# Turning gathered rows and weighed values by transposing transfers of 16-bit halves, in an attention and mixture-of-experts block

## The chip, the cores and the metric

The kernel runs on one core of one Trainium2 chip. A core has a matrix engine (TensorE, PE in the profile, with weight loads shown as PEld), a vector engine (DVE), a scalar engine (ACT), GpSimd (POOL) and a queue engine (SP) that here only issues DMAs. Each engine takes its own instructions in order and waits on semaphores for the others. The metric is the device time of one execution in microseconds, as a median over several runs.

## The reference

The block normalizes x (16 sequences of 256 tokens, 256 features, float32), and adds causal attention and a mixture of experts, both computed on the same normalized rows, to x.

```python
x = L0_attn_hidden_states                                  # (16, 256, 256)
xn = _layernorm(x, axis=-1)
# attention: 16 heads of 16, rotary positions
qkv = jnp.einsum('bsd,ed->bse', xn, w_qkv) + b_qkv
q = q * cos + _rotate_half(q) * sin                        # k likewise
scores = jnp.einsum('bhqd,bhkd->bhqk', q, k) / norm        # masked to j <= i
out = jnp.einsum('bhqk,bhkd->bhqd', softmax(scores), v)
# experts: 8 of them, inner width 512, weights from a router
probs = jax.nn.softmax(xn @ router_w.T, axis=-1)
w = _top_p_weights(probs, 0.9)                             # 0 for experts not kept
for e in range(8):
    y = (silu(xn @ gate_w[e].T) * (xn @ up_w[e].T)) @ down_w[e].T
    moe = moe + y * w[:, e:e + 1]
x = x + out + moe
```

## The kernel before

It has two stages.

**Attention.** Tokens lie in 32 tiles of 128; a sequence b has two of them (NQ = 2). A sequence takes 8 steps (PPS = 8): step i works on one pair of heads p of one chunk c of four heads, so there are 128 steps. A step multiplies queries with keys (products, tile s), takes the maxima of its rows on DVE (maxima, L593, which writes top), and, LAG = 11 steps later, does the same products the other way round (tile st) with the maximum folded in, and exponentiates them on ACT (probabilities, pr). Every second step four heads are weighed: weigh (L625) multiplies pr by the values into a PSUM tile o, whose row 16 of each head's 32 is the sum of the weights, and copies it to oT on ACT. One step later finish (L641) turns oT by two TensorE transposes into the PSUM tile ot, takes the reciprocal rs of the sums and the product at on DVE, and POOL adds at to xs. Between these, prep_jobs prepares the next sequence: prep_norm (L422 on) normalizes a tile into xn on ACT and stores it to the DRAM tensor rows; prep_xnT turns it; prep_qk, prep_v, rotation and prep_turn make queries, keys and values. The router's parts (router, L509) are taken one a step from an iterator, todo; the last of them go on to dispatch, which finds the slots of the first experts' tokens and gathers their rows.

The tensor rows holds, for each token, 256 normalized features and 8 expert weights, 1,056 bytes.

**Experts.** Each expert has room for 1,472 tokens (CAP), in 12 blocks of 128 (the last one of 64), worked off in four groups of up to three blocks. For a group, fetch gathers the rows of its blocks by an indirect DMA of POOL into xg, two groups ahead (AHEAD = 2). turn_in (L801) turns a block by two TensorE transposes into the PSUM tile xt and copies it to xT, on DVE or ACT by turns. expand (L813) multiplies xT by gate and up weights into gu, and makes hT. contract multiplies by the down weights into py, scales by the token's weight into ys, and scatters ys into out by an indirect DMA that adds. In one pass of the loop, for q = 0 to 3, come expand of group i, contract of block q of group i - 1, and turn_in of block q of group i + 1. load_expert(e + 1) puts three loads of 512 KB on SP at the first group of expert e; wd of an expert lies in one of two buffers. The search for slots (find, L309) multiplies selected rows into a tile seen and counts on DVE; eight waves of it (find_wave) run in the experts' stage. A last work item, the 33rd, takes an overfull expert's remaining tokens.

**PSUM.** Two pools: ps_m with two buffers (pq, pv, o, ot, xnt, top, upc, seen, xt, py) and ps_sc with three (s, st, gu).

**Order.** The program text gives priorities; the framework's scheduler writes the order of each engine's queue, and adds the semaphores. tc.issue_after and tc.high_priority bend that order in places.

Of the kernel before, what the change touches and what calls it, by code (L numbers as in the profile page):

```python
# [10 lines left out]
F32 = mybir.dt.float32  # L11
BF16 = mybir.dt.bfloat16
I32 = mybir.dt.int32
AF = mybir.ActivationFunctionType
# [9 lines left out]
MASKED = -3.0e38  # L24
CAP = 1472
# [6 lines left out]
def kernel(  # L32
# [27 lines left out]
    rt = rows[: NT * P, :].rearrange("(t p) c -> p t c", p=P)  # L60

# [247 lines left out]
    def find(h, js, to, numbers, token, name):  # L309
# [4 lines left out]
        for r in range(4):  # L314
            rows_r = slice(32 * r, 32 * r + 32)
            seen = ps_m.tile([P, 3, P + 2], F32, tag="m", name=f"seen_{name}_{r}")
# [6 lines left out]
            for i, j in enumerate(js):  # L323
                less = gat.tile([P, P], F32, tag="less", name=f"less_{name}", bufs=2)
# [22 lines left out]
    def find_wave(h, w):  # L347
# [9 lines left out]
        yield from find(h, js, holds, mine, to, f"{h}_{w}")  # L357
# [5 lines left out]
    def fetch_block(token, name, n=P):  # L363

        xg = gat.tile([P, D + E], F32, tag="xg", name=f"xg_{name}")
        nc.gpsimd.indirect_dma_start(  # L366
            out=xg[:n, :], out_offset=None, in_=rows,
            in_offset=bass.IndirectOffsetOnAxis(ap=token, axis=0),
        )
        return xg  # L370
# [21 lines left out]
    with tc.tile_pool(name="prep", bufs=2) as prep, tc.tile_pool(  # L392
# [21 lines left out]
        seqs, stored, sums, unturned, normed = {}, {}, {}, [], {}  # L414
# [7 lines left out]
        def prep_norm(b):  # L422

            normed[b] = []
            for qi in range(NQ):
                t = b * NQ + qi
                xn = prep.tile([P, D], F32, tag="xn", name=f"xn_{t}", bufs=6)
# [4 lines left out]
                stored[b] = nc.sync.dma_start(rt[:, t, :D], xn)  # L432
                normed[b].append(xn)

# [152 lines left out]
        def maxima(b, c, p, sc):  # L587

            for j in range(2):
                for qi in range(NQ):  # L590
                    lo, hi = (0, P) if qi == 0 else (P, W)
                    junk = probs.tile([P, 2 * P], F32, tag="junk", name=f"junk_{b}", bufs=2)
# [32 lines left out]
        def weigh(b, c, prs):  # L625
# [11 lines left out]
            oT = probs.tile([P, S], F32, tag="oT", name=f"oT_{b}_{c}", bufs=2)  # L637
            nc.scalar.copy(oT, o)
            return oT

        def finish(b, c, oT):  # L641
            ot = ps_m.tile([P, NQ, P], F32, tag="m", name=f"ot_{b}_{c}")
            for qi in range(NQ):
                nc.tensor.transpose(ot[:, qi, :], oT[:, ts(qi, P)], ident)
            ot = ot.rearrange("p q (h d) -> p (q h) d", d=HP)
# [37 lines left out]

        for t0 in (0, NQ):
# [29 lines left out]
        def dispatch():  # L714
# [3 lines left out]
            for w in range(AHEAD):  # L718
                yield from find_wave(0, w)
# [6 lines left out]
        while late < len(steps) or weighed or finished:  # L726
# [21 lines left out]
            if i < len(steps):  # L748
# [9 lines left out]
                for job in todo_now:  # L758
                    job()
                if i == PPS - 1:  # L760
# [23 lines left out]
            for _ in range(1 if i < len(steps) else 2):  # L784
                next(todo, None)
# [5 lines left out]
            for k in finished.pop(i, ()):  # L791
                finish(steps[k][0], steps[k][1], held.pop(k))
        at_once(todo)
# [213 lines left out]
```

## Time and profile before

| | us |
|---|---|
| median of 9 runs | 964.18 (960.73 to 969.74) |
| the profiled execution, its own time | 962.85 |
| its span, first to last instruction | 961.1 |
| granted TensorE clock, mean | 0.992 |

The page cuts the span into 40 slices of 24 us; each digit is a busy share in tenths:

```profile
PE   6988999999999999999999999999999999999996
...
DVE  3968788878787878551111433322111111212110
ACT  3254744565444444422222212112222222222221
POOL 5424233333433332434545344434544545446523
PEclk9979999999999999999999999999999999999999
DMA  7024100010200000112343322333432423424313
```

Attention ends near slice 17, at about 415 us, where DVE's digits fall from 8 to 1. The costliest groups that the change touches, by line, with busy time in all:

| line | what | count | mean ns | busy us |
|---|---|---|---|---|
| L644 | PE transposes ot of oT, 128x128 | 128 | 277 | 25.0 |
| L805 | PE transposes xt of xg, 128x128 | 176 | 276 | 34.1 |
| L805 | the same, 64 rows | 16 | 248 | 2.7 |
| L638 | ACT copy oT, 128x256 | 64 | 372 | 23.8 |
| L647 | DVE reciprocal rs, 128x8 | 64 | 200 | 12.8 |
| L649 | DVE product at, 128x128 | 64 | 291 | 18.6 |
| L806 | DVE copy xT, 128x256 | 57 | 424 | 24.2 |
| L806 | ACT copy xT, 128x256 | 32 | 364 | 11.6 |
| L318 | PE products seen, 128x130 | 208 | 290 | 27.2 |

Busy time counts overlapping instructions of one engine once, so it is below count times mean.

### The profile page before, as it was taken

The numbers are of one execution on the slowest core, as the hardware profiler recorded it, in microseconds if no ns is written. First come the engines' busy times: TensorE is split into PE (matmuls) and PEld (weight loads), VectorE is DVE, ScalarE is ACT, GpSimd is POOL, SyncE is SP. The second block draws the span as 40 slices with busy tenths as digits, with TensorE's granted clock in tenths as the row PEclk, the third lists the DMA queues.
The fourth block names the chain that finished last, engine by engine and source line by source line (L and its number), as shares of the span: only waits on it lengthen the run. The fifth ranks groups of instructions, "written<-read, shape, count | busy, mean of one in ns | idle before, by whom it ended". The sixth has DMA issues, their size and how long they took to land. (4 is left out here: it accounts for less than half of the span.)

```text
span 961.1 us, 17451 instructions
## 1 busy us (share of the span) xinstructions
PE 921.0 (96%) x6564; PEld 613.0 (64%) x6564; DVE 446.6 (46%) x2059; ACT 317.9 (33%) x606; POOL 400.5 (42%) x473
## 2 busy tenths in 40 slices
PE   6988999999999999999999999999999999999996
PEld 3555556566656666556766766666766667667675
DVE  3968788878787878551111433322111111212110
ACT  3254744565444444422222212112222222222221
POOL 5424233333433332434545344434544545446523
PEclk9979999999999999999999999999999999999999
DMA  7024100010200000112343322333432423424313
GB/s 248 13 89 155 59 13 13 14 57 25 89 24 14 13 13 14 42 56 48 56 105 55 89 58 43 66 79 55 90 72 45 108 53 60 106 51 91 56 20 39
DMA packets 46366, 57.53 MB, mean 60 GB/s; under 512 B 9313, under 2 KB 37601, under 8 KB 46273
## 3 DMA queue, kind: packets, MB, share of 16 engines
q0 software_dynamic: 19360, 29.81, 17.0%
q1 hardware_dynamic: 26912, 26.52, 8.6%
q8 instruction: 54, 0.88, 0.4%
q14 instruction: 40, 0.32, 0.1%
HBM read 32.14 MB, written 24.17 MB: 59 GB/s over the span
## 5 line engine op out<-in xcount | busy, mean ns | idle before, releaser
L871 POOL DMA_INDIRECT out<-ys,tokens x96 | 151.6, 1579 | 248.6 <-ACT ys L865 188.0
L825 DVE TENSOR_TENSOR hT<-act,gu 128x384 f32<-128x384 f32 (+2 forms) x132 | 69.9, 530 | 328.4 <-ACT act L824 328.3
L819 PE MATMUL gu<-xT,wg 128*128 128x384 f32 (+1 forms) x512 | 182.4, 477 | 0.0
L860 PE MATMUL py<-wd,hT 128*128 128x256 f32 (+1 forms) x768 | 181.8, 380 | 0.0
L819 PE MATMUL gu<-xT,wu 128*128 128x384 f32 (+1 forms) x512 | 181.0, 475 | 0.0
L593 DVE CUSTOM_DVE_ANT_0 junk<-s,mask 128x128 f32<-128x128 f32 (+1 forms) x512 | 152.5, 352 | 35.7 <-PE s L580 34.9
L860 PEld LDWEIGHTS py<-wd,hT 128*128 128x128 f32 (+1 forms) x768 | 141.7, 186 | 41.6 <-issue 3.8
L824 ACT ACTIVATE act<-gu 128x384 f32<-128x384 f32 (+2 forms) x132 | 62.2, 471 | 297.1 <-PE gu L819 292.0
L622 ACT ACTIVATE pr<-st 128x768 f32<-128x768 f32 x128 | 103.7, 812 | 115.7 <-PE st L617 114.7
L819 PEld LDWEIGHTS gu<-xT,wu 128*128 128x128 f32 x512 | 96.3, 190 | 59.4
L580 PE MATMUL s<-kT,qT 32*128 32x128 f32 (+1 forms) x1024 | 120.1, 353 | 3.8 <-ACT pr L622 2.7
L580 PE MATMUL st<-qT,kT 32*128 32x128 f32 (+1 forms) x1024 | 121.7, 361 | 2.0 <-DVE top L593 1.6
L366 POOL DMA_INDIRECT xg<-rows,tokens x96 | 94.2, 981 | 46.5 <-issue 21.0
L819 PEld LDWEIGHTS gu<-xT,wg 128*128 128x128 f32 x512 | 88.9, 190 | 37.1
L653 POOL TENSOR_TENSOR xs<-xs,at 128x128 f32<-128x128 f32 x64 | 29.8, 466 | 141.3 <-DVE at L649 141.3
L865 ACT ACTIVATE ys<-py,xg 128x256 f32<-128x256 f32 x96 | 45.4, 473 | 121.8 <-PE py L860 120.6
L580 PEld LDWEIGHTS st<-qT,kT 32*128 32x128 f32 x1024 | 68.9, 188 | 25.0 <-issue 18.4
L580 PEld LDWEIGHTS s<-kT,qT 32*128 32x128 f32 x1024 | 68.2, 188 | 9.1 <-ACT pr L622 3.8
L632 PE MATMUL o<-pr,va 128*32 128x256 f32 (+1 forms) x1024 | 57.0, 337 | 11.2 <-DVE at L649 10.0
L450 PE MATMUL pq<-wqkv_sb,xnT 128*128 128x512 f32 x128 | 63.9, 623 | 1.5 <-DVE logits L476 0.8
L489 POOL TENSOR_TENSOR kp<-qk,rot 128x256 f32<-128x256 f32 x32 | 24.2, 757 | 90.3 <-DVE rs L647 51.2
L611 POOL TENSOR_TENSOR qT<-qT,topT 128x256 f32<-128x256 f32 x64 | 50.8, 826 | 22.5 <-ACT topT L609 22.5
(156 smaller groups left out, 952.1 us busy)
## 6 DMA issues: line engine op xcount, KB each, us to landing
rows<-xn SPq DMA_DIRECT2D x32, 128.0 KB, 1.8
wg<-in_wg SPq DMA_DIRECT2D x8, 512.0 KB, 4.0
wu<-in_wu SPq DMA_DIRECT2D x8, 512.0 KB, 5.0
wd<-in_wd SPq DMA_DIRECT2D x8, 512.0 KB, 3.9
out<-xs SPq DMA_DIRECT2D x16, 256.0 KB, 2.2
xs<-in_x SPq DMA_DIRECT2D x3, 1024.0 KB, 11.3
rows<-zeros POOLq DMA_DIRECT2D x1, 1716.0 KB, 8.4
out<-zeros POOLq DMA_DIRECT2D x1, 1664.0 KB, 12.7
```

The lines of the kernel that those rows point to most:

```text
L366: nc.gpsimd.indirect_dma_start(out=xg[:n, :], out_offset=None, in_=rows, in_offset=bass.IndirectOffsetOnAxis(ap=token, axis=0),)
L450: nc.tensor.matmul(pq, xnT[:, c, ts(qi, P)], wqkv_sb[:, c, : 2 * D], start=(c == 0), stop=(c == DC - 1),)
L580: opened = nc.tensor.matmul(sc[:, j, to], left[rows, c, lhs], right[rows, c, lhs if first else slice(0, S)], start=first, stop=False, skip ...
L593: ins = nc.vector.tensor_tensor_reduce(junk[:, : hi - lo], sc[:, j, lo:hi], mask[:, 2 * P - (hi - lo) :], -1.0, -MASKED, ALU.add, ALU.min, ...
L611: nc.gpsimd.tensor_tensor(qT[:, c, :], qT[:, c, :], topT, ALU.add)
L622: nc.scalar.activation(pr, sc[:, :, :W], AF.Exp)
L632: nc.tensor.matmul(o[32 * hh : 32 * hh + 32, kc * P :], v[:, kc, 4 * c + hh, :], pr[:, j, : 2 * P] if kc == 0 else pr[:, j, 2 * P :], star ...
L819: nc.tensor.matmul(gu[:, j, :w], w_sb[:, c, ts(i, P)], xT[:, c, :w], start=(c == 0), stop=(c == DC - 1),)
L824: nc.scalar.activation(act[:, :w], gu[:, 0, :w], AF.Silu)
L825: nc.vector.tensor_tensor(hT[:, i, :w], act[:, :w], gu[:, 1, :w], ALU.mult)
L860: nc.tensor.matmul(py[:n, :], hT[:, i, k * P : k * P + n], d_sb[:, i, :], start=(i == 0), stop=(i == IC - 1),)
L871: ins = nc.gpsimd.indirect_dma_start(out=out, out_offset=bass.IndirectOffsetOnAxis(ap=token, axis=0), in_=ys[:n, :], in_offset=None, compu ...
```

## The change

Transposes on TensorE at two places give way to DMA transposes issued on SP. Such a transfer moves elements of 16 bits, so a float32 row is handled as its low and its high halves, side by side, and the halves are put together again by a copy behind the transfer.

- finish: oT is written by ACT as two planes of halves, [128, 2, 256]; a transfer turns it into half; POOL copies 17 of each head's 32 columns, halves interleaved, into the SBUF tile ot; rs and at read that.
- turn_in: rows keeps the 256 features as 256 low and then 256 high halves; a gather brings them into xg (16-bit type, same bytes); a transfer turns xg into half, six buffers; the DVE or ACT copy to xT interleaves the halves.
- store: the store to rows leaves prep_norm; a new function makes the planes of halves by an ACT copy and issues the store, for one waiting tile a step, in six of eight steps.
- find takes its pool as an argument; the eight waves in the experts' stage use ps_sc instead of ps_m.
- The router's next part is taken at the end of a step, behind weigh and finish, instead of ahead of them.
- 32 transposes of the identity (warm) stand at the start of TensorE's work.
- Fewer buffers: xn 6 to 5, less 2 to 1, junk 2 to 1.

```diff
+WARM = 32
...
+    halves = rows.bitcast(U16)
+    ht = halves[: NT * P, :].rearrange("(t p) c -> p t c", p=P)
...
-    def find(h, js, to, numbers, token, name):
+    def find(h, js, to, numbers, token, name, pool, tag):
...
-            seen = ps_m.tile([P, 3, P + 2], F32, tag="m", name=f"seen_{name}_{r}")
+            shape = [P, 4 * P] if pool is ps_m else [P, 2, 4 * P]
+            seen = pool.tile(shape, F32, tag=tag, name=f"seen_{name}_{r}")
+            seen = (seen if pool is ps_m else seen[:, 0, :])[:, : 3 * (P + 2)]
+            seen = seen.rearrange("p (i s) -> p i s", i=3)
...
-        xg = gat.tile([P, D + E], F32, tag="xg", name=f"xg_{name}")
+        xg = gat.tile([P, 2 * (D + E)], U16, tag="xg", name=f"xg_{name}")
         nc.gpsimd.indirect_dma_start(
-            out=xg[:n, :], out_offset=None, in_=rows,
+            out=xg[:n, :], out_offset=None, in_=halves,
...
-                stored[b] = nc.sync.dma_start(rt[:, t, :D], xn)
                 normed[b].append(xn)
+                unstored[t] = xn
+
+        def store(t):
+
+            half = prep.tile([P, 2, D], U16, tag="half", name=f"half_{t}")
+            nc.scalar.copy(
+                half, unstored.pop(t).bitcast(U16).rearrange("p (d h) -> p h d", h=2)
+            )
+            stored[t // NQ] = nc.sync.dma_start(
+                ht[:, t, : 2 * D], half.rearrange("p h d -> p (h d)")
+            )
...
-            oT = probs.tile([P, S], F32, tag="oT", name=f"oT_{b}_{c}", bufs=2)
-            nc.scalar.copy(oT, o)
+            oT = probs.tile([P, 2, S], U16, tag="oT", name=f"oT_{b}_{c}", bufs=2)
+            nc.scalar.copy(oT, o.bitcast(U16).rearrange("p (s h) -> p h s", h=2))
             return oT
 
         def finish(b, c, oT):
-            ot = ps_m.tile([P, NQ, P], F32, tag="m", name=f"ot_{b}_{c}")
-            for qi in range(NQ):
-                nc.tensor.transpose(ot[:, qi, :], oT[:, ts(qi, P)], ident)
-            ot = ot.rearrange("p q (h d) -> p (q h) d", d=HP)
+            half = probs.tile([P, 2, NQ * 4, HP], U16, tag="oh", name=f"oh_{b}_{c}", bufs=2)
+            nc.sync.dma_start_transpose(
+                half.rearrange("p h (q g) d -> p (h q) (g d)", q=NQ),
+                oT.rearrange("p h s -> p (h s)"),
+            )
+            ot = probs.tile([P, NQ * 4, HD + 2], F32, tag="ot", name=f"ot_{b}_{c}", bufs=2)
+            both = ot.rearrange("p g d -> p (g d)").bitcast(U16)
+            both = both.rearrange("p (g d h) -> p h g d", g=NQ * 4, h=2)
+            nc.gpsimd.tensor_copy(both[:, :, :, : HD + 1], half[:, :, :, : HD + 1])
...
+        warm = ps_sc.tile([P, 2, 4 * P], F32, tag="sc", name="warm")
+        for _ in range(WARM):
+            nc.tensor.transpose(warm[:, 0, :P], ident, ident)
...
+                if i % PPS not in (4, 5):
+                    for t in list(unstored)[:1]:
+                        store(t)
...
-            for _ in range(1 if i < len(steps) else 2):
-                next(todo, None)
             k = i - 1
...
                 finish(steps[k][0], steps[k][1], held.pop(k))
+            for _ in range(1 if i < len(steps) else 2):
+                next(todo, None)
...
-            tp = ps_m.tile([P, DC, P], F32, tag="m", name=f"xt_{name}_{i}")
-            for c in range(DC):
-                nc.tensor.transpose(tp[:, c, :n], xg[:n, ts(c, P)], ident[:n, :n])
+
+            half = hid.tile([P, 2 * DC, P], U16, tag="half", name=f"xt_{name}_{i}", bufs=6)
+            nc.sync.dma_start_transpose(half[:, :, :n], xg[:n, : 2 * D])
+            both = xT.rearrange("p c t -> p (c t)").bitcast(U16)
+            both = both.rearrange("p (c t h) -> p h c t", c=DC, h=2)
             (nc.scalar.copy if i % 2 else nc.vector.tensor_copy)(
-                xT[:, :, i * P : i * P + n], tp[:, :, :n]
+                both[:, :, :, i * P : i * P + n],
+                half.rearrange("p (h c) t -> p h c t", h=2)[:, :, :, :n],
             )
...
-                at_once(find_wave(*wave))
+                at_once(find_wave(*wave, ps_sc, "sc"))
```

More of the change, by code (lines that the diff above doesn't have):

```diff
@@ L13 @@
 I32 = mybir.dt.int32
+U16 = mybir.dt.uint16
 AF = mybir.ActivationFunctionType
@@ L323, in find @@
             for i, j in enumerate(js):
-                less = gat.tile([P, P], F32, tag="less", name=f"less_{name}", bufs=2)
+                less = gat.tile([P, P], F32, tag="less", name=f"less_{name}", bufs=1)
                 nc.vector.tensor_scalar(
@@ L345, with find_wave @@
     assert WAVES[-1] == (NB - 1,)
-    def find_wave(h, w):
+    def find_wave(h, w, pool, tag):
         js = WAVES[w]
@@ L356, in find_wave @@
         yield
-        yield from find(h, js, holds, mine, to, f"{h}_{w}")
+        yield from find(h, js, holds, mine, to, f"{h}_{w}", pool, tag)
     def at_once(parts):
@@ L412, in statistics @@
             )
-        seqs, stored, sums, unturned, normed = {}, {}, {}, [], {}
+        seqs, stored, sums, unturned, normed, unstored = {}, {}, {}, [], {}, {}
         def open_seq(b):
@@ L426, in prep_norm @@
                 t = b * NQ + qi
-                xn = prep.tile([P, D], F32, tag="xn", name=f"xn_{t}", bufs=6)
+                xn = prep.tile([P, D], F32, tag="xn", name=f"xn_{t}", bufs=5)
                 nc.scalar.activation(
@@ L591, in maxima @@
                     lo, hi = (0, P) if qi == 0 else (P, W)
-                    junk = probs.tile([P, 2 * P], F32, tag="junk", name=f"junk_{b}", bufs=2)
+                    junk = probs.tile([P, 2 * P], F32, tag="junk", name=f"junk_{b}", bufs=1)
                     ins = nc.vector.tensor_tensor_reduce(
@@ L718, in dispatch @@
             for w in range(AHEAD):
-                yield from find_wave(0, w)
+                yield from find_wave(0, w, ps_m, "m")
                 fetched[w] = fetch(*work[w])
@@ L792 @@
                 finish(steps[k][0], steps[k][1], held.pop(k))
+            for _ in range(1 if i < len(steps) else 2):
+                next(todo, None)
+        for t in list(unstored):
+            store(t)
         at_once(todo)
@@ L829, in weights_of @@
             if e < E:
-                return xg[:n, D + e : D + e + 1]
+                return xg.bitcast(F32)[:n, D + e : D + e + 1]
             picked = gat.tile([P, E], F32, tag="picked", name="picked", bufs=1)
             weight = gat.tile([P, 1], F32, tag="weight", name="weight", bufs=1)
-            nc.vector.tensor_tensor(picked, xg[:, D:], pick, ALU.mult)
+            nc.vector.tensor_tensor(picked, xg.bitcast(F32)[:, D:], pick, ALU.mult)
             nc.vector.tensor_reduce(weight, picked, AX.X, ALU.add)
@@ L941 @@
                     tile_rows = bass.ts(t, P)
-                    xg = gat.tile([P, D + E], F32, tag="xg", name=f"xg_o{e}")
-                    nc.sync.dma_start(xg, rows[tile_rows, :])
+                    xg = gat.tile([P, 2 * (D + E)], U16, tag="xg", name=f"xg_o{e}")
+                    nc.sync.dma_start(xg, halves[tile_rows, :])
                     xo = open_in(f"o{e}")
```

## The prediction

> **What bounds the kernel now.** I read first the busy times of the page, then busy times by stage, then the timeline of one stretch of each stage, then what the DMA queue waits for, last the durations of the nearest operations.
>
> ```profile
> PE 921.0 (96%) x6564; PEld 613.0 (64%) x6564; DVE 446.6 (46%) x2059; ACT 317.9 (33%) x606; POOL 400.5 (42%) x473
> ```
> ```profile
> 200.00:250.00 50.00, 47.61 (x592) 30.58 (x592) 37.38 (x192) 27.07 (x49) 17.72 (x27) 1.00 0.12 37
> ...
> 700.00:800.00 100.00, 100.00 (x388) 68.30 (x388) 18.84 (x38) 22.60 (x50) 48.12 (x39) 1.00 0.35 70
> ```
> The columns are PE, weight load, DVE, ACT, POOL, granted clock, DMA share, GB/s. TensorE is the bound in both stages: 95% busy in attention (about 25 to 415 us), 100% in the experts (about 415 to 955 us). But DVE is at 75% in attention and under 20% in the experts, so only attention has a second engine close behind.
>
> **What is removed.** Transposes on TensorE, in two places.
>
> ```profile
> 204.89 0.38 PE L644 MATMUL ot<-ident,oT 128*128 128x128 f32 x2
> ...
> 205.20 0.49 PE L580 MATMUL st<-qT,kT 32*128 32x128 f32 x4
> ...
> 205.47 0.20 DVE L647 RECIPROCAL rs<-ot 128x8 f32<-128x8 f32 x1
> ...
> 205.77 0.29 DVE L649 TENSOR_TENSOR at<-ot,rs 128x128 f32<-128x128 f32 x1
> ...
> 206.15 0.45 POOL L653 TENSOR_TENSOR xs<-xs,at 128x128 f32<-128x128 f32 x1 [4.00 <-DVE at L649]
> ```
> ```profile
> 759.73 1.89 PE L860 MATMUL py<-wd,hT 128*128 128x256 f32 x8
> 761.46 0.38 PE L805 MATMUL xt<-ident,xg 128*128 128x128 f32 x2
> 761.68 1.46 PE L819 MATMUL gu<-xT,wg 128*128 128x384 f32 x4
> 762.97 1.45 PE L819 MATMUL gu<-xT,wu 128*128 128x384 f32 x4
> ```
> Matmuls overlap, so the price of a pair is how far it pushes the next one: 205.20 - 204.89 = 0.31 us in attention (this holds for nearly all 64 pairs), 761.68 - 761.46 = 0.22 in the experts. That is 64 x 0.31 = 19.8 us, and 97 x 0.22 = 21.3, with 0.5 more for the eight pairs of 64 rows, which push 0.28: 41.6 us in all. Against the profiled execution (962.85 us, span 961.1 and 1.75 around it; the median of the runs is 1.3 above it) that alone would give 921.
>
> **What is added, and what hides it.**
>
> ```profile
> rows<-xn SPq DMA_DIRECT2D x32, 128.0 KB, 1.8
> ...
> xg<-rows,tokens POOLq DMA_INDIRECT x96, 2.8
> out<-ys,tokens POOLq DMA_INDIRECT x96, 3.8
> ```
> *Transfers.* 160 and one transposing transfers of 128 KB on SP. The trace has none. Bounds: the plain 128 KB store lands in 1.8 us, the scatter with addition in 3.8; I take 2.8, the gather, also 128 pieces of 1 KB spread over partitions. The Trainium skill (VectorE: DVE Perf Modes, "The three transpose paths") gives 1309 ns for one 128x128 16-bit square by DMA and prefers TensorE where PSUM will do; four such squares would be an estimate of 5.2 us, three blocks 15.7 us of a group of about 16, and the experts would gain next to nothing. The same skill (Advanced Engine Details and Errata, "X-Bar Transpose (TRN2)") calls such transfers as fast as ordinary ones, which would put them at the store's row; no row here decides between the two.
>
> *Finishing in attention.* The copy oT grows from 256 to 512 elements per partition.
> ```profile
> L611 POOL TENSOR_TENSOR qT<-qT,topT 128x256 f32<-128x256 f32 x64 | 50.8, 826 | 22.5 <-ACT topT L609 22.5
> ...
> L638 ACT COPY oT<-o 128x256 f32<-128x256 f32 x64 | 23.8, 372 | 57.3 <-PE o L632 57.0
> ...
> L505 ACT COPY qT<-qt 128x512 f32<-128x512 f32 x32 | 18.6, 580 | 0.8 <-PE qt L503 0.8
> ```
> So 372 becomes 580 ns, 64 x 0.21 = 13 us of ACT. POOL gets 64 copies of 272 halves: no less than its memset of 256 (0.31 us), no more than L611's 0.83; I take 0.55, 35 us. The stores' halving is 32 ACT copies of 512 elements, 0.58 each, 19 us. Over 390 us ACT goes from 27 to 31 of 50 and POOL from 18 to 22: covered. A late ACT copy can hold a pr, which TensorE's o needs: 0 to 32 x 0.58 = 19 us, I take 2, as ACT idles 23 of 50.
>
> The reciprocal now starts about 0.58 + 2.8 + 0.55 = 3.9 us after o, where it was some 2. The wait stands in DVE's queue: behind rs lie the next maxima (L593), and TensorE's products wait for these through three score banks. It costs nothing if the reciprocal is placed late enough. The scheduler does place by readiness: load_expert(0) stands at step 20 of the program, about 81 us by the first finishes (66.9 us at step 15, 84.0 at step 21), and the DMA queue issued it at 58.1. If its idea of a transfer is short, DVE stands. Bounds per finish: 0, and all the extra 1.9 us (122 us in all). DVE idles 12.6 of 50, 1.5 us per finish, which takes most of a small miss; I take 0.12, 8 us. One wait goes: ot held one of two PSUM buffers until at was done, and TensorE waited for that 12 us in attention (o 10.0 in 7 waits, xnt 2.1 in 3, by the table of waits). DVE's lateness stands behind these too and may come back elsewhere: gain 0 to 12, I take 6.
>
> *Turning in the experts.* Copies of 512 halves, 0.58 (ACT) to 0.69 us (DVE's 512-wide add), instead of 0.36 and 0.42: under 30 us on engines at 19 and 23 of 100. The transfers go on SP, where weights wait:
> ```profile
> SPq L658 <- POOL xs L653: 141.5, 16, 21.6
> ...
> SPq L87 <- PE xt L805: 85.2, 6, 16.2
> ```
> The wd load waits up to 16.2 us for the last contraction of the expert before. At 766.32 it goes out and TensorE reaches the next group at 769.08, 2.8 us later; three transfers behind it (4 issues of 0.37, 2.8, a copy 0.6: 4.9) would cost 2.1 at each of 6 changes, 13 us, up to 24 if they land in 3.8 and DVE has a backlog. I take 0: gathers run two groups ahead, six buffers hold two groups, so the transfers are ready long before wd is, and readiness orders the queue.
>
> *Slot search and the change of stages.* The search takes gu's three banks. Each tile holds one for a copy of 0.16 and three comparisons of 0.43, 1.45 us; later waves have py (5.2 us a group) to fill in, the first two have not: 8 x 1.45 less 8 x 6 x 0.12 of their own matmuls, 5.8 us at most. At 415 us the first xT copy waited for POOL's last xs (1.7 us): that chain grows by 2 and a transfer of 2.8 follows before the first gu. Bounds 0 to 11; I take 6.
>
> *Start.* 32 transposes of ident at some 0.25 us (the first four, at 6.18, took 1.09) run from 1.7 to about 9.7 us, 3.5 past the first real one; the first xnt, pq and pv took 0.45 + 1.88 + 0.89 = 3.2 longer than their next ones, at a granted clock of 1.00, so that much may come back. I take 0, bounds -3.2 to +3.5. One junk and one less buffer (same engine, in order), five xn of which a sequence uses two, gathers of the same 1,056 bytes a row: 0. The router's parts move behind rs and at on DVE and their store behind a transposing transfer on SP; what they make is needed only by the dispatch from step 115 on, so 0 before it, and at most one finish's 1.9 us there, which is in the 6.
>
> **Sum:** 962.85 - 41.6 - 6 + 8 + 2 + 6 = 931.3, say 931; its own range 916 to 955.
>
> **Rivals.**
> 1. *Nothing lost.* All 12 us of the bank's waits come back and no new wait shows: 962.85 - 41.6 - 12 = 909, up to 916 with some of the 6 at the change of stages. For it: the experts' slack; against: DVE at 75%. 0.12.
> 2. *SP order.* Transfers stand behind wd: 931 + 13 to 24, 944 to 955. For it: the 16 us waits; against: the reordering shown. 0.12.
> 3. *DVE stands in attention* (slower). Place: rs at each of 64 finishes. Gain left before it, 41.6 + 6 - 8 = 39.6 us, so it decides from 0.62 us each. At 1.2 us each, two thirds of the 1.9: 962.85 - 39.6 + 77 = 1000. For it: in-order queue, two added hops (DMA, POOL); against: DVE's idle time. 0.23.
> 4. *The transfers bound the experts.* At 5.4 us each, the longest gather, and none overlapping, a group needs 16.2 against 15.9 before: 32 x 0.3 = +10, attention even: 973. For it: DMA engines a third busy already; against: other transfers overlap. 0.10.
>
> **How the numbers follow.** Forecast 0.43, rivals as above. A change under 0.5% (4.8 us) can't be told from none here. Faster takes the forecast's 0.43 and the 0.12 of each of rivals 1 and 2: 0.67; same 0.05, that part of rival 3 that stays near its point of decision; slower the rest of it, 0.18, and rival 4's 0.10: 0.28. Below 912 and above 985 lie about 2 in 10: the upper end takes in rival 4 and the lower part of rival 3.
>
> **What would show it.** Right: no transposes on TensorE for ot and xt; an expert's four groups in some 60.9 us, where 63.5 is seen now; transfers landing in 2 to 4 us; eight attention steps in 22 to 23 us, now 23.7. Wrong: a wait of rs or junk for POOL's new copy, a share of DMA wait before gu, or a TensorE idle over 6 us near 415.

## The result, and the profile after

The changed kernel takes 1043.91 us (median of 10 runs, 1040.65 to 1048.77) against 964.18 us: a ratio of 1.083, with a 95% interval of 1.080 to 1.085. It is slower by some 80 us, where 931 was forecast. The kernel before itself has some executions of 975 to 979 us at a mean granted clock of 0.975 to 0.979, 4 of 13 beside e1 to e4 and 8 of 13 beside e13 and e14 (median there 975.19), so the ratios of those last two are not used.

The page of the kernel after, busy times and slices (its span is 1043.8 us, so a slice is 26 us):

```profile
PE 933.1 (89%) x6274; PEld 608.4 (58%) x6274; DVE 476.0 (46%) x2059; ACT 360.8 (35%) x638; POOL 436.4 (42%) x537
...
PE   6987696978788988888599999999999999999997
...
DVE  3866657876767777864331114343311111111111
...
PEclk8989879999899999976689999999999999999999
```

Most of TensorE's nines in attention (slices 2 to 16) have become sixes to eights, and the clock now shows sixes to eights in nine slices, where before only the third slice was below 9. TensorE has 290 fewer instructions and yet is busy 12 us longer.

Four marks cut each span into five stages that are nearly the same work in every kernel (a few products move across a mark with the order of the queues): the first and the last maxima on DVE, and the first and the last of the six loads of gate weights for experts 2 to 7, each of which waits for TensorE's last gate product two experts earlier. The spans by stage, in us, with the difference from before (from marks rounded to 0.1 us):

| kernel | start | attention | last maxima to end of expert 0 | five experts | rest | span | clock in the third stage |
|---|---|---|---|---|---|---|---|
| before | 24.1 | 367.2 | 88.7 | 335.2 | 145.9 | 961.1 | 0.98 |
| after | 29.7 (+5.6) | 448.2 (+81.0) | 104.9 (+16.1) | 320.2 (-15.0) | 140.8 (-5.0) | 1043.8 (+82.7) | 0.82 |
| e1_finish_only | -0.7 | +87.2 | +19.2 | 0.0 | +0.4 | +106.1 | 0.81 |
| e2_turn_only | +1.1 | +25.8 | +15.5 | -14.6 | -4.1 | +23.7 | 0.87 |
| e3_late_1 | +4.7 | +21.8 | +16.7 | -15.0 | -4.8 | +23.3 | 0.82 |
| e4_idle_transfer | +0.4 | +0.2 | +15.6 | 0.0 | +0.5 | +16.7 | 0.84 |
| e5_one_buffer | -1.0 | +28.6 | +3.1 | +0.7 | +0.5 | +31.9 | 0.98 |
| e6_two_buffers | +4.7 | +61.6 | +10.8 | -15.0 | -4.0 | +58.0 | 0.87 |
| e7_late_two | +4.9 | +18.6 | +12.3 | -15.0 | -4.4 | +16.4 | 0.83 |
| e8_best | +0.9 | +18.1 | +14.3 | -14.9 | -4.2 | +14.1 | 0.80 |
| e9_experts_part | +3.1 | +3.9 | +10.0 | -14.9 | -4.9 | -2.8 | 0.86 |
| e10_fill_later | +0.4 | +18.9 | +12.5 | -14.9 | -4.7 | +12.3 | 0.83 |
| e11_filled_14 | +1.2 | +7.4 | +7.5 | -14.9 | -4.5 | -3.3 | 0.91 |
| e12_filled_28 | +0.7 | +7.5 | +8.1 | -14.9 | -4.5 | -3.1 | 0.91 |
| e13_filled_68 | +0.8 | +7.1 | +10.7 | -14.9 | -4.9 | -1.3 | 0.95 |
| e14_fill_at_64 | +9.6 | +9.0 | +12.6 | -14.9 | -5.0 | +11.3 | 0.83 |

These are single profiled executions; a kernel's median can lie some us from its profiled one (e5's by 9, e4's by 4). The experts gain nearly what was forecast, 20 us. Attention loses four times that.

**What attention waits for.** Of the table of waits of the kernel after (waiting instruction, what ended the wait, us in all, times, longest):

```profile
POOL ot L667 <- DMA oh<-oT: 203.7, 51, 13.0
...
DVE rs L669 <- POOL ot L667: 97.4, 53, 8.0
...
PEld st L597 <- DVE top L610: 49.3, 48, 6.9
...
PE st L597 <- DVE top L610: 34.5, 34, 6.0
```

POOL's wait costs nothing by itself. The next line does: the reciprocal rs stands 97.4 us in DVE's queue, 71.5 of them ahead of the last maxima (57 finishes, 1.25 us each) and 26.0 behind them (7 finishes). The last two lines are TensorE's side: its products wait for maxima that stand behind rs. In the kernel before rs waited for TensorE, and all of it behind the last maxima, and the products waited 4.8 and 1.6 us:

```profile
DVE rs L647 <- PE ot L644: 7.2, 5, 2.0
...
PEld st L580 <- DVE top L593: 4.8, 17, 1.0
```

One finish in the timeline of the kernel after, one of the slow ones (start, us, engine, line, in brackets the idle time before it and what ended it):

```profile
216.96 0.58 ACT L655 COPY oT<-o 128x512 uint16<-128x512 uint16 x1
...
220.28 0.38 SPq L566 DMA_DIRECT2D rows<-wts  x1
...
220.77 1.19 SPq L660 DMA_TRANSPOSE oh<-oT  x1
...
224.55 0.50 POOL L667 COPY ot<-oh 128x272 uint16<-128x272 uint16 x1 [5.04 <-DMA oh<-oT]
225.09 0.20 DVE L669 RECIPROCAL rs<-ot 128x8 f32<-128x8 f32 x1 [3.28 <-POOL ot L667]
225.21 0.24 DVE L610 CUSTOM_DVE_ANT_0 junk<-s,mask 128x128 f32<-128x128 f32 x1
...
226.06 0.38 PE L597 MATMUL st<-qT,kT 32*128 32x128 f32 x2 [3.26 <-DVE top L610]
```

oT is ready at 217.54, but the transfer goes out at 220.77: in SP's queue it stands behind the router's store of weights, which waits for DVE. From oT to the reciprocal it is 7.5 us here. By the median of the 64 finishes the transfer goes out 0.06 us behind oT, and from oT to the reciprocal it is 4.30 us, where before it was 2.25; 7 transfers go out more than 2 us late. Here rs comes between maxima of one step, so TensorE waits 3.26 us for the maxima behind it.

### The profile page after: what moved, and what is told of

Same layout as the page of the kernel before. It is cut to its first block, busy times and chain, and to the rows that moved or that the text cites. A ratio compares the mean times of both kernels' runs of the same rounds, so it can differ in the third digit from the quotient of the medians.

```text
span 1043.8 us, 17154 instructions
## 1 busy us (share of the span) xinstructions
PE 933.1 (89%) x6274; PEld 608.4 (58%) x6274; DVE 476.0 (46%) x2059; ACT 360.8 (35%) x638; POOL 436.4 (42%) x537
## 2 busy tenths in 40 slices
DMA packets 131902, 78.12 MB, mean 75 GB/s; under 512 B 94848, under 2 KB 123136, under 8 KB 131808
## 5 line engine op out<-in xcount | busy, mean ns | idle before, releaser
L610 DVE CUSTOM_DVE_ANT_0 junk<-s,mask 128x128 f32<-128x128 f32 (+1 forms) x512 | 180.0, 351 | 32.4 <-PE s L597 20.0
L597 PE MATMUL st<-qT,kT 32*128 32x128 f32 (+1 forms) x1024 | 134.8, 382 | 36.6 <-DVE top L610 34.5
L597 PE MATMUL s<-kT,qT 32*128 32x128 f32 (+1 forms) x1024 | 129.7, 373 | 20.0 <-ACT pr L639 14.0
L853 PEld LDWEIGHTS gu<-xT,wg 128*128 128x128 f32 x512 | 97.0, 191 | 45.6 <-issue 4.2
L597 PEld LDWEIGHTS st<-qT,kT 32*128 32x128 f32 x1024 | 74.2, 199 | 78.7 <-DVE top L610 49.3
L667 POOL COPY ot<-oh 128x272 uint16<-128x272 uint16 x64 | 32.5, 508 | 203.7 <-DMA oh<-oT 203.7
L373 POOL DMA_INDIRECT xg<-rows,tokens x96 | 99.2, 1034 | 41.5 <-issue 27.7
L467 PE MATMUL pq<-wqkv_sb,xnT 128*128 128x512 f32 x128 | 67.9, 656 | 21.3 <-DVE logits L493 14.8
L839 DVE COPY xT<-xt 128x512 uint16<-128x512 uint16 x65 | 25.6, 437 | 96.5 <-PE gu L853 95.8
L649 PE MATMUL o<-pr,va 128*32 128x256 f32 (+1 forms) x1024 | 66.4, 376 | 0.1
L669 DVE RECIPROCAL rs<-ot 128x8 f32<-128x8 f32 x64 | 13.0, 203 | 97.7 <-POOL ot L667 97.4
```

Source lines behind the costliest of these rows:

```text
L373: nc.gpsimd.indirect_dma_start(out=xg[:n, :], out_offset=None, in_=halves, in_offset=bass.IndirectOffsetOnAxis(ap=token, axis=0),)
L467: nc.tensor.matmul(pq, xnT[:, c, ts(qi, P)], wqkv_sb[:, c, : 2 * D], start=(c == 0), stop=(c == DC - 1),)
L597: opened = nc.tensor.matmul(sc[:, j, to], left[rows, c, lhs], right[rows, c, lhs if first else slice(0, S)], start=first, stop=False, skip ...
L610: ins = nc.vector.tensor_tensor_reduce(junk[:, : hi - lo], sc[:, j, lo:hi], mask[:, 2 * P - (hi - lo) :], -1.0, -MASKED, ALU.add, ALU.min, ...
L649: nc.tensor.matmul(o[32 * hh : 32 * hh + 32, kc * P :], v[:, kc, 4 * c + hh, :], pr[:, j, : 2 * P] if kc == 0 else pr[:, j, 2 * P :], star ...
L853: nc.tensor.matmul(gu[:, j, :w], w_sb[:, c, ts(i, P)], xT[:, c, :w], start=(c == 0), stop=(c == DC - 1),)
```

## The experiments

**First four: which part loses.** Two theories stood against each other: W, that the reciprocal's wait in DVE's queue makes the loss, and T, that the transfers themselves disturb the other work.

e1_finish_only: the kernel before with the new weigh and finish, and one junk buffer; rows, turn_in, search, router and start as before.

```diff
-            nc.scalar.copy(oT, o)
+            nc.scalar.copy(oT, o.bitcast(U16).rearrange("p (s h) -> p h s", h=2))
...
-                nc.tensor.transpose(ot[:, qi, :], oT[:, ts(qi, P)], ident)
+            nc.sync.dma_start_transpose(...)
+            nc.gpsimd.tensor_copy(both[:, :, :, : HD + 1], half[:, :, :, : HD + 1])
```

> The kernel before with the new weigh and finish alone (transfer, POOL copy, rs and at from SBUF; one junk buffer to make room). Theory W (the reciprocal stands in DVE's queue before its data have landed, holds the maxima behind it, and TensorE stands): the attention loop grows by 65 to 85 us as in the changed kernel, 1025 to 1055 in all. Rival O (the other edits made it slow: stores by halves, start, search, router): the loop shrinks by the 20 us of the transposes, 940 to 960.

Measured: 1065.49 us, ratio 1.101 (1.093 to 1.108), above W's range. The loss is in this part (with the one junk buffer, which e5 takes apart), and is even larger without the experts' gain.

e2_turn_only: the kernel after with the finish, the search's pool, the router's place and the start of before; one junk and one less buffer stay.

```diff
-            half = probs.tile([P, 2, NQ * 4, HP], U16, tag="oh", name=f"oh_{b}_{c}", bufs=2)
-            nc.sync.dma_start_transpose(...)
+                nc.tensor.transpose(ot[:, qi, :], oT[:, ts(qi, P)], ident)
...
-                at_once(find_wave(*wave, ps_sc, "sc"))
+                at_once(find_wave(*wave))
```

> The kernel before with the experts' part alone: stores, gathers and rows in halves, turn_in by transfers; finish by TensorE, search on the old banks, no warm-up, router where it was. Theory W: the experts gain some 22 to 26 us as in the changed kernel and attention stays within 6 us (the stores' ACT copies), 938 to 952. Rival O: the stores or the change of stages eat it, 964 or more.

Measured: 989.11 us, 1.023 (1.016 to 1.031): a miss. The five experts gain their 15 us, but attention loses 25.8 without any transposing transfer in it. What was left there of the change was the buffers and the stores' copies; e5 takes that up.

e3_late_1: the kernel after, with POOL's copy, rs, at and the addition to xs (together settle) one step later, behind the maxima of that step.

```diff
+            return half
+
+        def settle(b, c, half):
...
+            for k, half in settled.pop(i, ()):
+                with tc.issue_after(behind.ins):
+                    settle(steps[k][0], steps[k][1], half)
```

> The changed kernel with the second half of finish (POOL copy, rs, at, addition to xs) put one step later, behind the four maxima of that step in DVE's queue. Theory W: the waits of rs for the copy fall from 97 us to under 30, the attention loop comes back from 448 to 360 to 385 us, 950 to 985 in all. Rival T (the transfers themselves slow the engines or the DMAs): no more than 15 us gained, 1030 or more.

Measured: 986.33 us, 1.019 (1.012 to 1.026). Attention falls from 448.2 to 389.0 us, rs waits 33.2 us instead of 97.4, both a little outside W's figures; ahead of the last maxima rs waits 8.4 us instead of 71.5. All transfers are still there, so 59 us of the loss come from when the reciprocal comes up in DVE's queue, and T falls.

e4_idle_transfer: the kernel before, with a transposing transfer of each oT, of the same size, that nothing reads.

```diff
+            half = probs.tile([P, 4, P], U16, tag="oh", name=f"oh_{b}_{c}", bufs=2)
+            nc.sync.dma_start_transpose(half, oT.bitcast(U16))
```

> The kernel before, with a transposing transfer of each oT added beside TensorE's transposes; nothing reads what it writes, and the order of every compute engine is as before. Theory W: within 8 us of before. Rival T: the 64 transfers cost most of the 80 us wherever they stand, 1010 or more.

Measured: 975.45 us, 1.0067 (1.002 to 1.011). Attention is 367.4 us, as before: 64 transfers that nobody waits for cost it nothing, and T falls for attention. Behind the last maxima, however, the stage is 15.6 us longer, in the profiled execution, at a clock of 0.84. There the two kernels differ by a few such transfers alone. But this execution took 979.50 us at a mean clock of 0.975, and the kernel before, without any such transfer, has executions like it (4 of 13 beside e4). So the lower clock is not shown to come from the transfers.

**The junk buffer, and the two together.** e5_one_buffer: the kernel before with one buffer for junk and one for less.

```diff
-                    junk = probs.tile([P, 2 * P], F32, tag="junk", name=f"junk_{b}", bufs=2)
+                    junk = probs.tile([P, 2 * P], F32, tag="junk", name=f"junk_{b}", bufs=1)
...
-                less = gat.tile([P, P], F32, tag="less", name=f"less_{name}", bufs=2)
+                less = gat.tile([P, P], F32, tag="less", name=f"less_{name}", bufs=1)
```

> The kernel before with one junk and one less buffer, nothing else. Theory J (a maximum that writes the buffer of the one before starts 0.12 us after that one's end instead of at once, as the traces show: 106.69 to 106.81 in the changed kernel, 202.12 to 202.12 in the one before): 512 x 0.12 = 61 us of DVE in the attention loop, which fills its idle time and adds 10 to 30 us to the loop, 974 to 996 in all. Rival N (same engine, in order: free, as was predicted): within 5 us of before.

Measured: 986.07 us, 1.0225 (1.020 to 1.025), with 28.6 us more in attention. The profiled execution took 994.73 us, 9 above the median; by the medians, 986.07 against 963.89, one buffer costs some 22 us. The timeline of DVE in the kernel before and in e5, a maximum, the read of its result, the next maximum:

```profile
201.90 0.29 DVE L593 CUSTOM_DVE_ANT_0 junk<-s,mask 128x128 f32<-128x128 f32 x1 [1.22 <-PE s L580]
202.12 0.08 DVE L593 DVE_READ_ACCUMULATOR2_ANT top<- 128x1 f32 x1
202.12 0.42 DVE L593 CUSTOM_DVE_ANT_0 junk<-s,mask 128x256 f32<-128x256 f32 x1
```
```profile
212.14 0.29 DVE L593 CUSTOM_DVE_ANT_0 junk<-s,mask 128x128 f32<-128x128 f32 x1 [1.55 <-PE s L580]
212.35 0.08 DVE L593 DVE_READ_ACCUMULATOR2_ANT top<- 128x1 f32 x1
212.47 0.42 DVE L593 CUSTOM_DVE_ANT_0 junk<-s,mask 128x256 f32<-128x256 f32 x1
```

With two buffers the next maximum starts together with the read, with one it starts 0.12 us after it. junk is never read; its only use is to be written. (e5 does not part junk from less; but less is written 104 times, 79 of them behind the first gate product, junk 512 times in attention.) A step has three such gaps between its four maxima: 128 x 3 x 0.12 = 46 us of DVE, of which its idle time swallows some.

e6_two_buffers: the kernel after with junk in two buffers and the stores' half in one.

```diff
-                    junk = probs.tile([P, 2 * P], F32, tag="junk", name=f"junk_{b}", bufs=1)
+                    junk = probs.tile([P, 2 * P], F32, tag="junk", name=f"junk_{b}", bufs=2)
```

> The changed kernel with two junk buffers (room from one half buffer less in the stores). If J and W both hold: the loop falls from 448 us by 15 to 45, 1000 to 1030 in all, the waits of rs stay above 70 us. If J is nothing beside W: 1038 to 1050.

Measured: 1019.80 us, 1.058 (1.055 to 1.061). Attention gets 19.4 us back; rs still waits 87.3 us. In this kernel all 57 reciprocals ahead of the last maxima stand ahead of the first maximum of a step, where in the kernel after 27 of them do and 30 stand between two maxima of one step. They still wait 67.1 us, and attention is still 61.6 us longer than before.

e7_late_two: e3_late_1 and e6_two_buffers together.

```diff
-                    junk = probs.tile([P, 2 * P], F32, tag="junk", name=f"junk_{b}", bufs=1)
+                    junk = probs.tile([P, 2 * P], F32, tag="junk", name=f"junk_{b}", bufs=2)
...
+            return half
+
+        def settle(b, c, half):
```

> The changed kernel with rs and at one step later and two junk buffers. J and W together: the loop at 347 to 365 us (367 before, less up to 20 for the transposes), 943 to 965 in all; the change of stages stays at some 48 us. Rival C (TensorE's granted clock is lower for another reason than its idle time): the loop stays above 380.

Measured: 978.22 us, 1.016 (1.012 to 1.020): a miss. Attention comes down to 385.8, 18.6 above before, where rival C had put it (above 380). e8, which is alike in attention (385.3), shows below where these us lie.

e8_best: e7_late_two, with less in two buffers too (and xn in four), the search on ps_m as before, and no transposes at the start.

```diff
-WARM = 32
+WARM = 0
...
-                at_once(find_wave(*wave, ps_sc, "sc"))
+                at_once(find_wave(*wave, ps_m, "m"))
```

> As e7_late_two, and two less buffers, four xn, the search on its old banks and no warm-up transposes. If the search on gu's banks made the change of stages long: it falls from 48 to 30 to 38 us; if the warm-up made the start long: first maxima at 24 to 25 us instead of 29; 918 to 948 in all. If neither: 943 to 965.

Measured: 977.63 us, 1.014 (1.010 to 1.018): again a miss. The start comes down from 29.0 in e7 to 25.0 us; of the edits, the 32 transposes are the one at that place. The third stage stays 14 us too long, so the search's banks don't make it long.

Where e8 still loses in attention shows the time of eight steps each, from the starts of their first maxima:

| steps | before | after | e8 | e14 |
|---|---|---|---|---|
| 8 to 16 | 26.2 | 26.7 | 24.8 | 24.2 |
| 16 to 24 | 24.7 | 37.7 | 31.3 | 30.9 |
| 24 to 32 | 25.3 | 31.8 | 33.7 | 25.7 |
| 32 to 40 | 24.4 | 30.7 | 27.5 | 28.1 |
| 40 to 48 | 22.1 | 24.1 | 22.0 | 21.7 |
| 48 to 56 | 24.4 | 31.0 | 23.2 | 23.2 |

From step 40 on e8 is about as fast as before, and no faster. The windows from the first maxima of step 40 to the last maxima, in before and in e8 (us, then busy time of PE, PEld, DVE, ACT and POOL, granted clock, DMA share, GB/s):

```profile
142.58:391.33 248.75, 238.52 (x2944) 153.55 (x2943) 199.12 (x1033) 124.12 (x214) 84.91 (x129) 1.00 0.09 28
```
```profile
160.17:410.30 250.13, 235.45 (x2874) 144.59 (x2872) 201.69 (x1036) 141.24 (x231) 107.90 (x174) 1.00 0.23 51
```

44 pairs of transposes are gone there, 13.6 us at 0.31 us each, but the stretch is as long, with 14.0 us of waits of rs left. What holds it there was not tested. In the hump, the timeline of POOL and SP in e8:

```profile
90.64 1.40 POOL L232 DMA_DIRECT2D rows<-zeros  x1 [0.33 <-POOL zeros L807]
```
```profile
97.15 6.87 SPq L660 DMA_TRANSPOSE oh<-oT  x2
```
```profile
105.86 0.50 POOL L670 COPY ot<-oh 128x272 uint16<-128x272 uint16 x1 [9.24 <-DMA oh<-oT]
```

Two fills of together 3.4 MB go out at 91 and 93 us, and the transfer issued at 97.15 has its reader start at 105.86, 8.7 us later; the median landing is 2.4 us.

**The experts' part alone.** e9_experts_part: the kernel before with rows in halves, stores' copies and turn_in by transfers; finish, search, router, start, junk and less as before, xn in five buffers.

```diff
+            half = hid.tile([P, 2 * DC, P], U16, tag="half", name=f"xt_{name}_{i}", bufs=6)
+            nc.sync.dma_start_transpose(half[:, :, :n], xg[:n, : 2 * D])
```

> The kernel before with the experts' part of the change alone, and with two junk and two less buffers: rows are stored as 16-bit halves, the gathered blocks are turned by transposing transfers; the weighed values are still turned by TensorE, the slot search keeps its banks, the router its place, no warm-up. Theory (the loss is the finish's wait and the one junk buffer; the experts' gain is real and apart from them): loop 367 to 375 us (the 32 half copies of 0.62 us lie on ScalarE, which has room), change of stages 27 to 32 us, experts 517 to 525 us, together 938 to 955 us, a ratio of 0.973 to 0.990 to the kernel before. Rival R (the experts' gain depends on the slot search's new banks, as the 535 us of the run e2_turn_only would say): experts 532 us or more, together 955 to 975 us, a ratio of 0.99 to 1.01.

Measured: 962.78 us, 0.9985 (0.996 to 1.001): no gain, and R's total. But its reason is not R's. The loads that mark expert after expert, in the kernel before, after, and in e9:

```profile
751.74 0.37 SPq L85 DMA_DIRECT2D wg<-in_wg  x1
...
815.22 0.37 SPq L85 DMA_DIRECT2D wg<-in_wg  x1
```
```profile
842.31 0.37 SPq L89 DMA_DIRECT2D wg<-in_wg  x1
...
902.95 0.37 SPq L89 DMA_DIRECT2D wg<-in_wg  x1
```
```profile
756.64 0.37 SPq L88 DMA_DIRECT2D wg<-in_wg  x1
...
817.28 0.37 SPq L88 DMA_DIRECT2D wg<-in_wg  x1
```

An expert takes 63.48 us before and 60.64 in both others, whatever the search's banks. (The time from the first gate product to the end, which the expectation calls the experts, is 543.4 us before, 517.4 after and 536.3 in e9, but it compares unlike things: of the search's 208 products 148, 112 and 160 lie behind that point.) Of the 20 us gained, 17 are lost again ahead of the load for expert 2: 3.1 at the start, 3.9 in attention and 10.0 in the third stage. e9's windows around its first gate product at 421.97 (columns as above; in the two between 434 and 446 TensorE is busy 6.00 us too, at 0.50):

```profile
416.00:422.00 6.00, 3.35 (x55) 1.62 (x43) 1.88 (x7) 2.25 (x5) 0.91 (x2) 1.00 0.55 127
422.00:428.00 6.00, 6.00 (x18) 3.78 (x18) 2.34 (x12) 2.05 (x2) 0.91 (x2) 0.54 0.28 61
428.00:434.00 6.00, 6.00 (x19) 3.38 (x19) 2.92 (x22) 0.27 (x1) 0.00 (x0) 0.50 0.10 32
...
446.00:452.00 6.00, 6.00 (x14) 3.32 (x13) 1.45 (x5) 0.98 (x2) 2.94 (x4) 0.69 0.16 45
452.00:458.00 6.00, 6.00 (x22) 4.02 (x22) 1.78 (x4) 2.01 (x4) 1.94 (x2) 1.00 0.66 139
```

TensorE idles 2.65 of 6 us, its longest wait being 1.61 us ahead of the product; then the clock is halved for some 27 us, by the windows' means, though TensorE has no idle moment in them. Busy digits don't show it; the length of four gate products does: 2.77 us at 446.18, in the halved stretch, and 1.45 at 450.55, behind it.

e10_fill_later: e8_best, with the zero fills written at step 64 of the program instead of step 24.

```diff
-                if i == 3 * PPS:
+                if i == 8 * PPS:
```

> The kernel of e8_best with the two zero fills at step 64 instead of step 24; the load of the first expert's weights stays at step 20. In e8_best eight attention steps took 31.3 and 33.7 us from step 16 to 32, 27.5 to 40, and 22 to 24 later. Theory Z (the transposing transfers wait behind the fills' traffic, and their readers with them): steps 24 to 40 fall to 23 to 26 us per eight, and a hump of 28 us or more for eight steps appears between steps 64 and 88; the total stays within 10 us of e8_best's 977. Rival L (the load of the weights or the state of the loop at that place makes the hump): steps 24 to 40 keep 27 to 34 us, and none appears behind step 64. Rival P (the two together make it): steps 24 to 40 fall and none appears behind 64; the loop falls to 375 us or less, the total to 962 to 970 us.

Measured: 974.45 us, 1.011 (1.006 to 1.015), with the hump as in e8. It decides nothing: the fills still went out at 91.6 and 94.4 us, since the scheduler orders by readiness and they depend on nothing late.

**The pause ahead of the first product.** e11_filled_14 and e12_filled_28: e9 with transposes on TensorE that nothing reads, 4 behind the last finish but one, and 10 or 24 behind the last.

```diff
+            if b == B - 1 and c >= CH - 2:
+                fill = ps_sc.tile([P, 2, 4 * P], F32, tag="sc", name=f"fill_{c}")
+                for _ in range(10 if c == CH - 1 else 4):
+                    nc.tensor.transpose(fill[:, 0, :P], oT[:, :P], ident)
```

> The kernel of e9_experts_part with 14 more transposes on TensorE that nothing reads, 4 behind the last finish but one and 10 behind the last, where TensorE waited 0.7 and 1.6 us ahead of the first gate product and the granted clock then stood at 0.50 from 422 to 446 us. Theory K (the experts' gain of some 22 us is there, and the pause ahead of the first product gave 14 of it back through the clock): the clock stays at 0.95 or more in the 30 us after the first product, the experts take 518 to 526 us, together 944 to 953 us, a ratio of 0.978 to 0.989. Rival N (the clock falls whatever is done in this pause, or it is not what costs the 14 us): experts 532 us or more, together 958 to 968 us, a ratio of 0.994 to 1.004.

> The same with 24 behind the last finish in place of 10: at 0.11 to 0.16 us each they last 2.6 to 3.9 us, over the whole pause. Theory K: the clock stays up at least as surely as with 10, and the time is that of e11_filled_14 plus 0 to 2.5 us, 944 to 955 us; if 10 were too few to hold the clock, this one alone falls to 944 to 955 us. Rival N: 960 to 970 us, the transposes' own time on top of e9's 962.8.

Measured: 960.46 us, 0.997 (0.994 to 1.000), and 960.09 us, 0.994 (0.992 to 0.997). e12 is the one version that, by the ratios used here, is measurably faster than both kernels, by 0.6% against before. It is not the 944 to 955 of theory K: another wait of 1.76 us (for DVE) then stood ahead of the first product, and the clock fell behind it, for some 17 us instead of 27. Within e11's own 12 executions time and clock go together: 957.61 us at 0.978, 970.50 at 0.963; 0.015 of 958 us is 14 us, the spread is 13.

e13_filled_68: e12 with 10 more such transposes behind each of the four groups of the search's third wave.

```diff
+            if name == "0_2":
+                for _ in range(10):
+                    nc.tensor.transpose(fill[:, 0, :P], to[:, :P], ident)
```

> The kernel of e12_filled_28 with 10 more transposes that nothing reads behind each of the four groups of comparisons of the search's third wave, where TensorE still waited 1.8 us for VectorE ahead of the first gate product, and the clock then stood at 0.50 to 0.69 from 428 to 446 us. Theory K (TensorE's pauses ahead of the first product bring the clock down, and this gives 8 to 14 us of the experts' gain back): the clock stays at 0.9 or more in the 24 us after the first product, the experts take 517 to 524 us, the change of stages 29 to 33 us, together 946 to 956 us, a ratio of 0.981 to 0.992. Rival N (the clock falls there whatever TensorE does, as it did with 14 and 28): the experts 526 us or more, together 960 to 968 us.

Measured: 961.00 us. Windows of e13, before and behind its first product at 442.1:

```profile
398.00:404.00 6.00, 3.66 (x48) 2.50 (x46) 3.73 (x25) 2.45 (x4) 3.46 (x4) 1.00 0.24 69
404.00:410.00 6.00, 5.63 (x40) 3.12 (x41) 0.18 (x2) 1.67 (x4) 2.77 (x4) 0.52 0.01 3
410.00:416.00 6.00, 6.00 (x69) 4.36 (x68) 3.46 (x22) 2.03 (x3) 1.33 (x2) 0.63 0.00 0
...
440.00:446.00 6.00, 6.00 (x40) 4.22 (x38) 4.41 (x33) 0.00 (x0) 2.88 (x3) 1.00 0.32 67
446.00:452.00 6.00, 6.00 (x20) 3.60 (x19) 2.21 (x12) 0.98 (x2) 3.68 (x4) 1.00 0.61 130
```

With the pauses filled the clock stays at 1.00 behind the first product, as K said; N falls on this point. K's total falls too: an earlier pause (3.66 of 6 us busy, at the end of attention) was now followed by some 10 us at half clock, and the filling is work of its own.

**The fills.** e14_fill_at_64: e8_best, with the fills tied to the maxima of step 64.

```diff
-                if i == 3 * PPS:
-                    with tc.issue_after(sums[4 * NQ - 1].ins):
+                if i == 8 * PPS:
+                    with tc.issue_after(behind.ins):
```

> The kernel of e8_best with the two zero fills tied to the maxima of step 64 (in e10_fill_later they were only written later, and still went out at 92 and 94 us). Theory Z: steps 24 to 40, 33.7 and 27.5 us in e8_best, fall to 23 to 28 and 22 to 26 us, a transfer of the weighed values no longer takes 9 us there, and a hump of 27 us or more for eight steps appears between steps 64 and 80; steps 16 to 24 (31.3 us, beside the load of the first expert's weights at 62 to 70 us) stay. Rival L (the fills don't make the hump): steps 24 to 40 keep 27 us or more each, and none appears behind 64.

Measured: 977.35 us. The tie holds in the program's order only, and the fills went out at 16.8 and 19.9 us, ahead of attention: neither theory's place, but a test all the same. Steps 24 to 32 take 25.7 us instead of 33.7, and attention 9 us less; the start takes 9 us more. So the fills make that part of the hump, as Z said; 16 to 24 and 32 to 40 stay.

## Why the prediction was wrong, by its own steps

**Removed transposes.** The experts' term was right in size: 2.6 us an expert forecast (63.5 to 60.9), 2.84 measured, 20 us in the last two stages. Attention's 19.8 us did not come. In the kernel after TensorE idles 77.6 us of attention (21.5 before), so it was no longer the bound there; but from step 40 on e8 has few such waits and shows no gain either.

**Transfers.** Taken as 2.8 us; they landed in 2.4 (oT) and 3.1 us (xg), by median. The estimate of 5.2 us from the Trainium skill (VectorE: DVE Perf Modes, "The three transpose paths") was too long for both; the other page, Advanced Engine Details and Errata, "X-Bar Transpose (TRN2)", which calls them as fast as ordinary transfers, is closer: the store of 128 KB landed in 1.9 us. Their issue takes 1.19 us on SP, where 0.37 was taken. So rival 4 had no ground, and rival 2 neither: the load of wd waits 12.0 us in all for TensorE's py, the gate products wait only 0.7 us in all, and an expert gained its 2.84 us.

**The wait in DVE's queue: the step that failed.** The reciprocal came 2.05 us later behind oT than before (4.30 instead of 2.25, by median), near the 1.9 of the prediction. What failed is the next step: that DVE's idle time, 1.5 us per finish, would take most of this and leave 0.12 us per finish, 8 us. In attention alone rs waited 1.25 us per finish, 71.5 us. The waits of rs ahead of the last maxima, in the kernel after, in e6 and in e3:

```profile
DVE rs L669 <- POOL ot L667: 71.5, 46, 8.0
```
```profile
DVE rs L669 <- POOL ot L667: 67.1, 42, 6.0
```
```profile
DVE rs L672 <- POOL ot L670: 8.4, 7, 2.9
```

The idle time did not help, because rs stood ahead of maxima for which TensorE then waited. Whether it stands between two maxima of one step or between two steps is not what decides, by e6; coming up a step later, when the copy of POOL is mostly done, does, by e3, which gives 59 of attention's 81 us back. A few finishes were later still: in the one shown, 3.2 of 7.5 us are the transfer's wait behind the router's store in SP's queue, and the prediction had that store behind the transfer, not ahead of it. Rival 3 named the place, and its 1.2 us per finish was close; its 1000 us was too low, as it held nothing for the buffers, the change of stages and the start. The lower clock adds to it: of attention's 81 us, 56 are more idle time of TensorE and 25 are more busy time.

**The bank's waits.** A gain of 6 us was taken. TensorE's wait of 10.0 us for o is gone (0.1), but its wait in front of pq rose from 1.5 to 21.3 us, 14.8 of them for DVE's copy logits: DVE's lateness came back elsewhere, as the prediction had allowed.

**One junk buffer: "same engine, in order: 0".** It costs 28.6 us of attention alone in e5's profiled execution, some 22 by the medians, and 19.4 beside the waits (e6). The trace of before had no row with one buffer, so the bounds had to reach up to some gap per maximum; I gave none. The parts don't add up: 59.2 (late) and 19.4 (buffers) apart, 62.4 together.

**Change of stages.** 6 us with bounds of 0 to 11; the third stage became 16.1 longer. Its windows in before, in e4 and in the kernel after:

```profile
391.30:480.00 88.70, 85.97 (x553) 57.44 (x554) 29.36 (x143) 25.41 (x49) 40.62 (x43) 0.98 0.24 52
```
```profile
391.90:496.30 104.40, 99.87 (x553) 66.03 (x554) 29.40 (x143) 25.53 (x49) 40.79 (x43) 0.84 0.27 53
```
```profile
477.90:582.80 104.90, 89.41 (x491) 61.66 (x492) 29.60 (x139) 27.64 (x48) 43.59 (x49) 0.82 0.41 77
```

In e4 the same 553 matmuls keep TensorE busy for 13.9 us more, and it idles 1.8 us more: nearly all of the 15.6 us is the lower clock (104.4 x 0.16 less 88.7 x 0.02 is 14.9, from clocks of two digits). The kernel after has the lower clock too, but TensorE is busy only 3.4 us more, with 62 matmuls fewer, and idles 15.5 us instead of 2.7. Here the failed step comes back: the last seven finishes stand in this stage, and the search's copies and comparisons stand behind their reciprocals in DVE's queue.

```profile
DVE rs L669 <- POOL ot L667: 26.0, 7, 7.2
```
```profile
511.94 1.63 PE L325 MATMUL seen<-order,holds 32*128 32x130 f32 x6 [7.05 <-DVE part L329]
```

This is the idle time of over 6 us that the prediction had named as a sign of being wrong. How the 16 us divide between clock and waits was not separated. e13, at a clock of 0.95, is busy 93.7 us, its filling included. What sets off the halving isn't settled: a pause of TensorE comes before it, but the kernel before has one too (waits of 0.92 and 0.52 us at the start of this stage; 0.80 in one window) and is back at 1.00 two windows later.

**Start.** 0 was taken, bounds -3.2 to +3.5; it was 5.6. Without the 32 transposes it is 0.9 (e8), so they delay the first real products and give nothing back. (Without them the start still varies: -1.0 to +1.2, 3.1 in e9, and 9.6 in e14, which has the fills there.)

**Still open.** Some 9 us of attention in e14, in steps 16 to 24 (beside the load of the first expert's weights) and 32 to 40; why the removed transposes gain nothing from step 40 on; what sets off the halving of the clock; and how to keep the clock through the whole change of stages.

## What to carry to other kernels

A step that is moved from one engine to a chain over three (ACT to SP to POOL to DVE) is priced at the instruction where the chain ends: find what stands behind it in that engine's queue, and who waits for that, and let it come up only when its data have landed (here one step later). A scratch output that nobody reads can still need two buffers where instructions follow each other closely, as junk did. When a gain shows in the steady part and not in the total, compare equal work by marks, and read the granted clock in windows of a few us before looking for a wait.

## What the hardware showed that I had not expected

- The granted clock stood at 0.50 for some 27 us after a wait of 1.61 us, with TensorE busy 6.00 of every 6.00 us meanwhile (e9). The Trainium skill (TensorE: Matmul & The Clock Gate, "What's actually happening") has the clock halved after at least one idle window of about 3.4 us and restored after at least one busy window of that length. The halving to one half agrees. No wait here was 3.4 us long (TensorE idled 2.65 of 6 us, in pieces), and 27 us are some eight such windows, which the page does not lead one to expect; the measurement decides here.
- In attention the mean clock fell from 0.99 to 0.91 as TensorE's idle time grew from 21.5 to 77.6 us, and with it 3,944 matmuls took 370.6 us of busy time where 4,040 had taken 345.7. Here the waits on other engines were paid a second time in the clock.
- Maxima on DVE that write the same buffer start 0.12 us after the read of the one before, those that alternate start with it. Whether the engine or a semaphore holds them isn't told apart.
- The transposing transfers are made of small pieces: from before to after packets rose from 46,366 to 131,902, those under 512 bytes from 9,313 to 94,848. Attention didn't mind 64 of them that nobody waited for (e4).
- Behind 3.4 MB of zero fills on another queue a transposing transfer of e8 took up to 5.9 us to land and 2.8 to issue, where 2.4 and 1.2 are the medians.
